# Layer 0 of a graph network: the end of the mixing moved from the counting stage into the graph products

## The chip, the cores and the metric

The kernel runs on one core of a Trainium2 chip. The metric is the device time of one execution in microseconds (us), as the median of several runs. The whole program has four layers; the change touches the first of them (layer 0) alone, which takes some 740 of the 3743 us.

The names of the engines in the profile: PE is the matrix engine (PEld its loads of weights), DVE the vector engine, ACT the scalar engine, POOL the GpSimd engine, SP the engine that only issues transfers. Each engine works off its instructions strictly in the order in which they stand in its queue.

## The reference

There are 3125 nodes with 256 features, and 100000 edges. Layer 0 begins like this (cut to what matters):

```
xn = layernorm(x)
x  = x + gnn(xn, edges) + mix(xn)
x  = x + ffn(layernorm(x))

gnn:  deg = number of edges of each node (src), loops added
      agg = sum over edges and loops of xn[dst] * deg[src]**-.5 * deg[dst]**-.5
      return relu(agg @ W.T + b)

mix:  z = rmsnorm(xn) ;  q, k, v = split(z @ w_qkv)          # 4 heads of 32
      q = softmax(q over a head's features) * 32**-.5 ;  k = softmax(k over nodes and memory)
      context = k . v ;  out = rmsnorm((q . context) @ w_out + b_out) * g_out
      return out + xn
```

## The kernel before

The nodes stand in 25 blocks of 125 (P); `x` and `xn` lie in the on-chip memory as 125 x 25 x 256, and most steps work on pieces of four blocks (`PIECES`: six pieces of 500 nodes and one of 125). The order in which the instructions of an engine stand is decided when the program is built, by a scheduler that goes by the dependences, the order in which the source issues them, and its own estimates of durations. `tc.issue_after(i)` keeps what stands inside it behind the instruction i on the same engine.

Layer 0 has four stages.

1. *Preparation* (`prep`). The edges are loaded, places in the edge list are searched (`junk`, `cnt`, `st`, and at line 404 `idx1`), and `x` is normalised piece by piece into `xn` (`l0_norm`) and turned into `xt` (`l0_unit`). When all of it is done and its memory is free, the edge records are gathered (line 456).

2. *Counting, with the mixing between* (`l0_first`: `counts` and `l0_mix_by_pieces`, interleaved by `together`, which always advances the part whose progress is smaller). For each of 25 target blocks b, `counts` builds one-hot rows of the edges (DVE, lines 507 and 510), multiplies them on PE (line 512), copies the result out with ACT (line 515, seven copies a block), turns it in four rounds through one bank of the accumulation memory (PE line 525, copied out in turn by DVE line 179 and ACT line 181), adds up degrees (line 530) and stores the turned counts in the memory off chip, `cnt_d[b]`, one row of blocks after another.
   The mixing first makes the context (`context`: the maxima of k, the sums over 25 blocks, and at its end `ctx_w`, which is the context times `w_out`, called `m2`). Then, for each piece, come the queries (lines 946 to 957), turned into `qt` (lines 961 and 964), and then what is called *the tail* here: for each block one matmul `qt` x `m2` (line 970), the addition of `b_out` (971), a square with its sum (ACT, 973); for each piece a square root (974), 975 and 976; for each block the scaling (979); for each piece `x += xn` (983, held behind line 957 by `issue_after`) and `x += t` (984).

3. *Weights of the graph layer* (`l0_gnn`, its first loop). `acc` = `xn` is overwritten by `xt` x W, scaled (PE line 279; DVE 616 or ACT 614), and then split into three bf16 parts, `y3` (lines 619 to 622).

4. *Graph products* (`l0_gnn`, its second loop). The 25 blocks of counts are read back (`cb`, line 629 through the helper lines 172 and 173 on SP's queue) in groups of 6, 6, 6 and 7 sources, in 12 buffers. For each group there are 25 steps h: 3 x m matmuls of 125 x 125 by 125 x 256 in bf16 into one bank (line 634), then the addition of the bank to `acc` on DVE (636). There are four such banks (`bank()`), shared with all other matmuls of the stage. In the last group a step also ends its block: lines 639 and 640, and for each finished piece, one piece later, the normalisation (lines 216 to 225), the turning (267, 179, 181) and the gates of the next part (279, 305, 1115, 1116).

Of the kernel before, what the change touches and what calls it, by code (L numbers as in the profile page):

```python
# [12 lines left out]
F32 = mybir.dt.float32  # L13
# [3 lines left out]
BF = mybir.dt.bfloat16  # L17
AF = mybir.ActivationFunctionType
OP = mybir.AluOpType
# [4 lines left out]
N = 3125  # L24
D = 256
# [92 lines left out]
PIECES3 = [(i, PW) for i in range(0, 4 * PW, PW)] + [(i, LW) for i in range(4 * PW, N, LW)]  # L118
NT = -(-N // 32) * 32
STORED = (4, 8, 12, 16, 20, 23, 25)  # L120
SOURCES = (6, 6, 6, 7)


class Net:
# [466 lines left out]
    def l0_gnn(self):  # L591

        nc = self.nc
        with ExitStack() as s:
            sb = s.enter_context(self.pool("g0_sb"))
            wk = s.enter_context(self.pool("g0_wk", 2))
            yb = s.enter_context(self.pool("g0_y", side="right"))
            w, bias = self.l0_w
            di = sb.tile([P, NB], F32, name="di")
            nc.scalar.activation(di, self.deg, AF.Sqrt)  # L600
            nc.vector.reciprocal(di, di)
            f = sb.tile([P, NB], F32, name="f")
            nc.vector.tensor_mul(f, di, self.len16)
            acc = self.xn
            y3 = yb.tile([P, NB, 3, D], BF, name="y3")
            for i, c in PIECES:
                b0, b1 = i // P, (i + c) // P
                for b in range(b0, b1):
                    if (b - b0) % 2 == 0:
                        ps = self.bank()  # L610
                    v = ps[:P, (b - b0) % 2 * D:][:, :D]
                    self.mm_tok(v, self.xt, b, w)
                    if b % 2:
                        nc.scalar.activation(acc[:, b, :], v, AF.Copy, scale=f[:, b:b + 1])
                    else:
                        nc.vector.tensor_scalar(acc[:, b, :], v, f[:, b:b + 1], None, op0=OP.mult)
                y, r = acc[:, b0:b1], wk.tile([P, 4, D], F32, name="r")[:, :b1 - b0]
                h0, h1, h2 = (y3[:, b0:b1, k, :] for k in range(3))
                nc.scalar.copy(h0, y)
                nc.vector.tensor_sub(r, y, h0)  # L620
                nc.scalar.copy(h1, r)
                nc.vector.tensor_sub(h2, r, h1)
            b0 = 0
            for m in SOURCES:
                cf = []
                for b in range(b0, b0 + m):
                    cb = wk.tile([P, N], BF, name="cb", bufs=2 * SOURCES[0])
                    self.move(nc.sync, cb, self.cnt_d[b])
                    cf.append(cb)
                for h in range(NB):  # L630
                    ps = self.bank()
                    for k in range(m):
                        for j in range(3):
                            nc.tensor.matmul(ps[:P, :D], cf[k][:, h * P:(h + 1) * P], y3[:, b0 + k, j, :],  # L634
                                             start=(k == 0 and j == 0), stop=(k == m - 1 and j == 2))
                    nc.vector.tensor_add(acc[:, h, :], ps[:P, :D], acc[:, h, :])  # L636
                    if b0 + m == NB:
                        t = acc[:, h, :]
                        nc.vector.scalar_tensor_tensor(t, t, di[:, h:h + 1], bias[:P], op0=OP.mult, op1=OP.add)
                        nc.vector.scalar_tensor_tensor(self.x[:, h, :], t, 0.0, self.x[:, h, :],  # L640
                                                       op0=OP.max, op1=OP.add)
                        if h % 4 == 3 or h == NB - 1:
                            self.arrive(h // 4 * PW)
                b0 += m
# [163 lines left out]
                nc.sync.dma_start(self.cnt_d[ds(b, 1)].rearrange("o p n -> (o p) n"), new)  # L808


    def context(self, sb, wk, w, wo, mem, share):


        nc = self.nc
# [47 lines left out]
        m2 = sb.tile([128, D], F32, name="ctx_w")  # L862
        nc.vector.tensor_scalar(m2, ps[:, :D], rz, 32 ** -0.5, op0=OP.mult, op1=OP.mult)
        return m2

# [36 lines left out]
                self.l0_norm(i, w)  # L902
                self.l0_unit(wk, r, i, w)

    def l0_first(self):

        with ExitStack() as s:
            csb = s.enter_context(self.pool("c_sb"))
            cwk = s.enter_context(self.pool("c_wk", 2))
            msb = s.enter_context(self.pool("m0_sb"))  # L910
            mwk = s.enter_context(self.pool("m0_wk", 2))
            pt = s.enter_context(self.pool("c_pt", 2, space=PSUM))
            px = s.enter_context(self.pool("c_px", 1, space=PSUM))
            py = s.enter_context(self.pool("c_py", 1, space=PSUM))
            mix = self.l0_mix_by_pieces(msb, mwk)
            next(mix)
            self.together([self.counts(csb, cwk, pt, px, py), mix])

    def l0_mix_by_pieces(self, sb, wk):
# [11 lines left out]
        bo = self.load_b(sb, "L0_mix_b_out")  # L931
        go = self.load_b(sb, "L0_mix_g_out")
# [5 lines left out]
        m2 = yield from self.context(sb, wk, w, wo, (mk, mv, mkt), 0.4)  # L938
        for i, c in PIECES:
            b0, n = i // P, c // P  # L940

            def part(f):
                return 0.4 + 0.6 * (i + f * c) / N

            ps = self.bank()
            for j in range(n):
                self.mm_tok(ps[:P, j * 128:(j + 1) * 128], self.xt, b0 + j, w[:, :, :128])
            q = wk.tile([P, 16, 32], F32, name="q")
            pq = ps[:P, :n * 128].rearrange("p (g d) -> p g d", d=32)
            qm = wk.tile([P, 16], F32, name="qm")  # L950
            nc.vector.tensor_reduce(qm[:, :4 * n], pq, axis=AX.X, op=OP.max)
            nc.vector.tensor_sub(q[:, :4 * n], pq, qm[:, :4 * n, None].to_broadcast([P, 4 * n, 32]))
            nc.scalar.activation(q[:, :4 * n], q[:, :4 * n], AF.Exp)
# [10 lines left out]
            nc.scalar.copy(qt[:, :c], ps[:, :c])  # L964
            yield part(0.6)
            t = wk.tile([P, 4, D], F32, name="t", bufs=1)
            ss = wk.tile([P, 4], F32, name="ss")
            for j in range(n):
                ps = self.bank()
                nc.tensor.matmul(ps[:P, :D], qt[:, j * P:(j + 1) * P], m2, start=True, stop=True)  # L970
                nc.vector.tensor_add(t[:, j, :], ps[:P, :D], bo[:P])
                sq = wk.tile([P, D], F32, name="sq")
                nc.scalar.activation(sq, t[:, j, :], AF.Square, accum_out=ss[:, j:j + 1])
            nc.scalar.activation(ss[:, :n], ss[:, :n], AF.Sqrt)
            nc.vector.tensor_scalar(ss[:, :n], ss[:, :n], 1e-12, 1.0 / 16, op0=OP.max, op1=OP.mult)
            nc.vector.reciprocal(ss[:, :n], ss[:, :n])
            yield part(0.9)
            for j in range(n):
                nc.vector.scalar_tensor_tensor(t[:, j, :], t[:, j, :], ss[:, j:j + 1], go[:P],
                                               op0=OP.mult, op1=OP.mult)  # L980
            v = self.x[:, b0:b0 + n, :]
            with self.tc.issue_after(weighed.ins):
                nc.vector.tensor_add(v, v, self.xn[:, b0:b0 + n])
            nc.vector.tensor_add(v, v, t[:, :n])
            yield part(1.0)

    def gen_l0_gnn(self):
        nc = self.nc
# [1898 lines left out]
    def run(self):  # L2887
# [5 lines left out]
        self.l0_first()  # L2893
        with self.pool("f0_g") as sb:
            self.l0_gates(sb)
            self.l0_gnn()
            first.__exit__(None, None, None)
            self.open_right()
            self.l0_ffn(True)
# [80 lines left out]
```

## Time and profile before

| | us |
|---|---|
| median of 3 runs (3740.36 to 3747.85) | 3740.75 |
| the profiled execution, its own time | 3745.47 |
| its span in the profile | 3743.2 |
| preparation, up to the first gather of records | 0 to 74.5 |
| counting and mixing; the last counts are stored at | 74.5 to 449.7 |
| weights, split and start of the products | 449.7 to 491.5 |
| products, groups of 6, at full rate | 491.5 to 631 |
| products, last group of 7 | 631 to 707 |

A row of groups by line reads: line, engine, operation, out<-in with partitions x elements, count | busy time, mean duration in ns | idle time of the engine just before them, and who ended it. A row of stretches reads: the stretch, its length, then for PE, PEld, DVE, ACT and POOL the busy time and (in brackets) the number of instructions, then the granted clock of the matrix engine as a share of the full one, the share of the transfer engines and GB/s. In the order of time a row begins with start and duration. A matmul in f32 shows as two records. Durations of instructions that follow each other closely overlap by some 0.08 us, so that a full queue advances by a little less than the duration shown.

### The profile page before, as it was taken

Reading aid. Unit: us, or ns where it says so; the run is one execution under the profiler, and the core shown is the slowest. Engines: PE = TensorE matmul, PEld = TensorE weight load, DVE = VectorE, ACT = ScalarE, POOL = GpSimd, SP = SyncE. Lnnn points to the kernel's source line nnn. Section 1 sums busy time; section 2 is a strip of 40 time slices with the busy share of each in tenths; the row PEclk is TensorE's granted clock in tenths of the full one; section 3 lists DMA queues with packets and bytes.
Section 4 is the critical chain, followed back from the end, with each engine's and each line's share of the span. In section 5 each row is a group of like instructions: output and inputs, shape, how many; then the busy total and the mean of one; then the engine's idle time right before and its main releaser. Section 6 shows DMA issues by size and latency. Waiting matters only on the chain. (4 is left out here: it accounts for less than half of the span.)

```text
span 3743.2 us, 61732 instructions
## 1 busy us (share of the span) xinstructions
PE 3319.3 (89%) x22027; PEld 2299.3 (61%) x22027; DVE 2406.5 (64%) x8119; ACT 1641.0 (44%) x3742; POOL 720.2 (19%) x702
## 2 busy tenths in 40 slices
PE   1888899789988979999998889998999999999978
PEld 1676699678866555555556677876663443444436
DVE  6878633875546673379246677886376666677663
ACT  3367510022225522222335566653247655556562
POOL 2000000054420340000003777772000000100011
PEclk9887699899989969999998899998999999999989
DMA  4144552346642110000003554545003222222135
GB/s 130 32 126 130 142 144 65 95 149 191 179 107 59 37 40 2 18 9 15 11 1 109 141 140 137 140 128 176 12 9 84 66 56 64 57 59 62 30 118 168
DMA packets 215084, 321.85 MB, mean 86 GB/s; under 512 B 51373, under 2 KB 158904, under 8 KB 214766
## 3 DMA queue, kind: packets, MB, share of 16 engines
q1 hardware_dynamic: 165308, 231.04, 21.5%
q0 software_dynamic: 40672, 83.85, 8.3%
q10 hardware_dynamic: 8786, 2.91, 0.4%
q8 instruction: 177, 2.90, 0.3%
q14 instruction: 141, 1.16, 0.1%
HBM read 248.17 MB, written 78.08 MB: 87 GB/s over the span
## 5 line engine op out<-in xcount | busy, mean ns | idle before, releaser
L2442 ACT ACTIVATE xn<-xn,us 125x1000 f32<-125x1000 f32 (+2 forms) x400 | 399.9, 1036 | 145.6 <-DVE z L2447 140.4
L2447 DVE SCALAR_TENSOR_TENSOR z<-xn,us,cs 125x1000 f32<-125x1000 f32 (+2 forms) x400 | 397.4, 1026 | 101.6 <-PE acc L2463 61.3
L2025 POOL DMA_INDIRECT hg<-hx_d,idx x405 | 403.5, 996 | 168.0 <-issue 99.3
L2463 PE MATMUL acc<-z,xr 125*32 125x500 f32 (+1 forms) x2800 | 368.7, 548 | 18.3 <-DVE z L2447 17.5
L1932 ACT ACTIVATE o<-ky,rest_d 128x50 bf16<-128x50 bf16 (+2 forms) x1190 | 302.9, 340 | 172.0 <-DVE ky L1923 149.3
L285 PE MATMUL ps<-xt,w 128*128 128x500 f32 (+1 forms) x672 | 274.7, 556 | 2.7 <-DMA w<-in_L_ffn_W_dram 1.6
L1655 DVE SCALAR_TENSOR_TENSOR x<-ps,lg,x 125x256 f32<-125x256 f32 x200 | 93.3, 483 | 245.4 <-PE ps L279 245.3
L2052 PE MATMUL acc<-hg,to 128*125 128x256 f32 x810 | 226.2, 422 | 11.5 <-DVE to L2048 10.7
L2463 PEld LDWEIGHTS acc<-z,xr 125*32 125x32 f32 x2800 | 100.1, 110 | 205.3 <-issue 116.9
L2463 PE MATMUL acc<-z,ones 125*32 125x500 f32 (+1 forms) x1400 | 224.9, 542 | 0.0
L634 PE MATMUL ps<-y,cb 125*125 125x256 bf16 x1875 | 210.6, 275 | 7.1 <-DVE xn L636 2.6
L634 PEld LDWEIGHTS <-cb 125*125 125x125 bf16 x1875 | 207.9, 138 | 7.7 <-issue 7.7
L285 PEld LDWEIGHTS ps<-xt,w 128*128 128x128 f32 x672 | 124.4, 198 | 116.0 <-issue 102.5
L279 PE MATMUL ps<-wo,h 128*125 128x256 f32 x800 | 187.8, 386 | 3.6 <-ACT h L1649 2.6
L1644 ACT ACTIVATE h<-ps,bnb,bng 128x500 f32<-128x500 f32 (+1 forms) x112 | 80.5, 722 | 248.6 <-PE ps L285 248.6
L2052 PEld LDWEIGHTS acc<-hg,to 128*125 128x125 f32 x810 | 156.5, 204 | 43.6 <-DVE to L2048 20.6
L279 PEld LDWEIGHTS ps<-wo,h 128*125 128x125 f32 x800 | 142.9, 187 | 65.8 <-ACT h L1649 43.5
L285 PE MATMUL ps<-h,w 128*128 128x500 f32 (+1 forms) x448 | 179.2, 541 | 1.4 <-ACT h L1644 1.0
L512 PE MATMUL t<-ky,lo 128*128 128x75 bf16 (+4 forms) x1251 | 140.6, 253 | 35.4 <-ACT ct L515 19.9
L515 ACT ACTIVATE ct<-t 125x500 bf16<-125x500 f32 (+4 forms) x175 | 137.0, 830 | 75.7 <-PE t L512 73.2
L285 PE MATMUL pl<-xbt,w 128*128 128x256 f32 x560 | 152.5, 402 | 10.0 <-ACT xbt L1271 9.2
L206 ACT ACTIVATE rstd_t<-rstd_t 125x4 f32<-125x4 f32 (+3 forms) x86 | 17.1, 202 | 301.6 <-DVE rstd_t L205 300.5
(696 smaller groups left out, 6902.9 us busy)
## 6 DMA issues: line engine op xcount, KB each, us to landing
w<-in_L_ffn_w_dram SPq DMA_DIRECT2D x70, 512.0 KB
cs<-ctt_d SPq DMA_DIRECT2D x100, 218.8 KB
lb<-low_d SPq DMA_DIRECT2D x76, 256.0 KB
w<-in_L_ffn_w_dram SPq DMA_DIRECT2D x18, 1024.0 KB
cnt_d<-cd SPq DMA_DIRECT2D x25, 683.6 KB
cb<-cnt_d SPq DMA_DIRECT2D x25, 683.6 KB
ctt_d<-ct SPq DMA_DIRECT2D x5, 2734.4 KB
cs<-ctt_d SPq DMA_DIRECT2D x50, 164.1 KB
```

What stands on the lines that cost most here:

```text
L279: self.nc.tensor.matmul(ps, xt[:, h, b * P:(b + 1) * P], w[:, h, :], start=(h == 0), stop=(h == k - 1))
L285: self.nc.tensor.matmul(ps, w[:, h, :], xt[:, h, i:i + n], start=(h == 0), stop=(h == k - 1))
L512: nc.tensor.matmul(t[:, w * 25 * r:(w + 1) * 25 * r], lo[:, :, n % 4], ky[:, :25 * r, n % 4], start=(j == 0), stop=(j == ws[w0 + w][2] - 1))
L515: nc.scalar.activation(ct[:, :, w0 * r:(w0 + m) * r].rearrange("p h (w r) -> p w h r", r=r), t[:P, :m * 25 * r].rearrange("p (w h r) -> p ...
L634: nc.tensor.matmul(ps[:P, :D], cf[k][:, h * P:(h + 1) * P], y3[:, b0 + k, j, :], start=(k == 0 and j == 0), stop=(k == m - 1 and j == 2))
L1655: nc.vector.scalar_tensor_tensor(self.x[:, b, :], ps[:P, :D], g[:, b, e:e + 1], self.x[:, b, :], op0=OP.mult, op1=OP.add)
L1932: nc.scalar.activation(o1[:, k], ky[:, :, i], AF.Copy, scale=rest[:, k, n + i:n + i + 1])
L2025: nc.gpsimd.indirect_dma_start(out=hg[:, j, :], out_offset=None, in_=hx, in_offset=bass.IndirectOffsetOnAxis(ap=idx[:, c0 + j - CF:c0 + j ...
L2052: nc.tensor.matmul(acc, to, hg[:, j, :D], start=(c == first[kind]), stop=(c == last[kind]))
L2442: nc.scalar.activation(t[:, :n], (tail if one else rows)[:P, h, :n], AF.Relu, bias=us[:, 2, b, h:h + 1], scale=us[:, 0, b, h:h + 1])
L2447: made.append(nc.vector.scalar_tensor_tensor(zs[h], t[:, :n], us[:, 1, b, h:h + 1], c, op0=OP.add, op1=OP.mult).ins)
L2463: mm = nc.tensor.matmul(out[q:q + 32, :w], left, zs[h0 + j][:, k * w:k * w + w], start=(b == 0), stop=(b == NB - 1), tile_position=(0, q))
```

## The change

- The tail of the mixing leaves the counting stage. All seven turned queries are kept in one tile of 128 x 3125 (`qt` in a new pool `m0_r`), with `m2`, `b_out` and `g_out`.
- In the graph products a generator, `l0_mixed`, is advanced once after each step h: four advances issue one block each (matmul, addition, square), the fifth issues the rest of the piece (root, scaling, `x += t`). With 32 advances it ends in the second group. The square is now written in bf16.
- `x += xn` becomes `l0_base` and is issued in the first loop of `l0_gnn`, before `acc` overwrites `xn`; there it stands in no `issue_after`.
- The sources come in five groups of five, in 9 buffers.

```diff
-SOURCES = (6, 6, 6, 7)
+SOURCES = (5, 5, 5, 5, 5)
...
             for i, c in PIECES:
+                self.l0_base(i, c)
                 b0, b1 = i // P, (i + c) // P
...
+            kept, *rest = self.l0_kept
+            mixed = (y for i, c in PIECES for y in self.l0_mixed(wk, i, c, kept[:, i:i + c], *rest, "r"))
...
-                    cb = wk.tile([P, N], BF, name="cb", bufs=2 * SOURCES[0])
+                    cb = wk.tile([P, N], BF, name="cb", bufs=2 * SOURCES[0] - 1)
...
                     nc.vector.tensor_add(acc[:, h, :], ps[:P, :D], acc[:, h, :])
+                    next(mixed, None)
...
-            qt = wk.tile([128, PW], F32, name="qt")
+            qt = kept[:, i:i + c] if keep else wk.tile([128, PW], F32, name="qt")
             nc.scalar.copy(qt[:, :c], ps[:, :c])
+            if keep:
+                yield part(1.0)
+                continue
...
+    def l0_base(self, i, c):
+        v, vn = (t[:, i // P:(i + c) // P] for t in (self.x, self.xn))
+        self.nc.vector.tensor_add(v, v, vn)
+
+    def l0_mixed(self, wk, i, c, qt, m2, bo, go, name="t"):
+        nc, b0, n = self.nc, i // P, c // P
+        t = wk.tile([P, 4, D], F32, name=name)
+        ss = wk.tile([P, 4], F32, name="ss")
+        for j in range(n):
+            ps = self.bank()
+            nc.tensor.matmul(ps[:P, :D], qt[:, j * P:(j + 1) * P], m2, start=True, stop=True)
+            nc.vector.tensor_add(t[:, j, :], ps[:P, :D], bo[:P])
+            sq = wk.tile([P, D], BF, name="sq")
+            nc.scalar.activation(sq, t[:, j, :], AF.Square, accum_out=ss[:, j:j + 1])
+            yield 0.4 + 0.6 * (i + j * P) / N
+        nc.scalar.activation(ss[:, :n], ss[:, :n], AF.Sqrt)
+        nc.vector.tensor_scalar(ss[:, :n], ss[:, :n], 1e-12, 1.0 / 16, op0=OP.max, op1=OP.mult)
+        nc.vector.reciprocal(ss[:, :n], ss[:, :n])
+        for j in range(n):
+            nc.vector.scalar_tensor_tensor(t[:, j, :], t[:, j, :], ss[:, j:j + 1], go[:P],
+                                           op0=OP.mult, op1=OP.mult)
+        v = self.x[:, b0:b0 + n, :]
+        nc.vector.tensor_add(v, v, t[:, :n])
+        yield 0.4 + 0.6 * (i + c) / N
```

In `run` the new pool is opened on the right side around `l0_first` and `l0_gnn`, and closed after the products.

More of the change, by code (lines that the diff above doesn't have):

```diff
@@ L808, in gen_counts, with context @@
                 nc.sync.dma_start(self.cnt_d[ds(b, 1)].rearrange("o p n -> (o p) n"), new)
-    def context(self, sb, wk, w, wo, mem, share):
+    def context(self, sb, wk, w, wo, mem, share, keep=None):
         nc = self.nc
@@ L861, in context @@
         nc.tensor.matmul(ps[:, :D], ct, wo[:, 0, :], start=True, stop=True)
-        m2 = sb.tile([128, D], F32, name="ctx_w")
+        m2 = (keep or sb).tile([128, D], F32, name="ctx_w")
         nc.vector.tensor_scalar(m2, ps[:, :D], rz, 32 ** -0.5, op0=OP.mult, op1=OP.mult)
@@ L903, in l0_prepare, with l0_first @@
                 self.l0_unit(wk, r, i, w)
-    def l0_first(self):
+    def l0_first(self, keep):
         with ExitStack() as s:
@@ L914, in l0_first, with l0_mix_by_pieces @@
             py = s.enter_context(self.pool("c_py", 1, space=PSUM))
-            mix = self.l0_mix_by_pieces(msb, mwk)
+            mix = self.l0_mix_by_pieces(msb, mwk, keep)
             next(mix)
             self.together([self.counts(csb, cwk, pt, px, py), mix])
-    def l0_mix_by_pieces(self, sb, wk):
+    def l0_mix_by_pieces(self, sb, wk, keep=None):
         nc, a = self.nc, self.a
@@ L930, in l0_mix_by_pieces @@
         wo = self.load_w(sb, "L0_mix_w_out", eng=nc.scalar)
-        bo = self.load_b(sb, "L0_mix_b_out")
-        go = self.load_b(sb, "L0_mix_g_out")
+        bo = self.load_b(keep or sb, "L0_mix_b_out")
+        go = self.load_b(keep or sb, "L0_mix_g_out")
         yield 0
@@ L937, in l0_mix_by_pieces @@
         self.searched = None
-        m2 = yield from self.context(sb, wk, w, wo, (mk, mv, mkt), 0.4)
+        m2 = yield from self.context(sb, wk, w, wo, (mk, mv, mkt), 0.4, keep)
+        if keep:
+            kept = keep.tile([128, N], F32, name="qt")
+            self.l0_kept = kept, m2, bo, go
         for i, c in PIECES:
@@ L962, in l0_mix_by_pieces @@
                                     self.ident[:P, :P])
-            qt = wk.tile([128, PW], F32, name="qt")
+            qt = kept[:, i:i + c] if keep else wk.tile([128, PW], F32, name="qt")
             nc.scalar.copy(qt[:, :c], ps[:, :c])
+            if keep:
+                yield part(1.0)
+                continue
             yield part(0.6)
[L966 to L981, printed above, removed]
-            with self.tc.issue_after(weighed.ins):
-                nc.vector.tensor_add(v, v, self.xn[:, b0:b0 + n])
@@ L984, in l0_mix_by_pieces @@
-            nc.vector.tensor_add(v, v, t[:, :n])
-            yield part(1.0)
+            with self.tc.issue_after(weighed.ins):
+                self.l0_base(i, c)
+            yield from self.l0_mixed(wk, i, c, qt, m2, bo, go)
+    def l0_base(self, i, c):
[21 more added lines that the diff above has]
+        yield 0.4 + 0.6 * (i + c) / N
@@ L2892, in run @@
         self.l0_w = self.load_w(gw, "L0_gnn_W"), self.load_b(gw, "L0_gnn_b")
-        self.l0_first()
+        mixed = self.pool("m0_r", side="right")
+        self.l0_first(mixed.__enter__())
         with self.pool("f0_g") as sb:
@@ L2896, in run @@
             self.l0_gnn()
+            mixed.__exit__(None, None, None)
             first.__exit__(None, None, None)
```

## The prediction

> **What bounds the kernel now.** First the stretches of layer 0, one row per stage (columns: PE, PEld, DVE, ACT, POOL busy, granted clock, transfer share, GB/s).
>
> ```profile
> 0.00:74.50 74.50, 15.16 (x58) 9.80 (x58) 46.59 (x164) 30.53 (x99) 13.71 (x24) 1.00 0.50 135
> ...
> 278.60:387.30 108.70, 85.88 (x865) 71.49 (x866) 91.57 (x247) 79.18 (x194) 0.42 (x2) 0.70 0.44 124
> 387.30:449.70 62.40, 49.07 (x427) 40.54 (x426) 45.58 (x117) 39.59 (x109) 0.21 (x1) 0.69 0.58 151
> ...
> 491.50:631.00 139.50, 139.49 (x1278) 139.49 (x1278) 30.68 (x73) 0.00 (x0) 0.00 (x0) 1.00 0.35 90
> 631.00:707.00 76.00, 73.22 (x649) 71.78 (x647) 59.12 (x226) 4.12 (x11) 0.00 (x0) 0.98 0.15 44
> ```
>
> To see: where the tail of the mixing runs (278.6 to 449.7), no engine is full; PE, DVE and ACT wait for each other. The products are PE and nothing else (1278 matmuls in 139.5 us, 0.109 each), until in the last group DVE is at 78%. Next, the groups of the tail between 276 and 446, and one line of the waits there:
>
> ```profile
> L970 PE MATMUL ps<-ctx_w,qt 128*125 128x256 f32 x50 | 23.5, 591 | 1.1 <-ACT qt L964 1.1
> L979 DVE SCALAR_TENSOR_TENSOR t<-t,ss,L_mix_g_out 125x256 f32<-125x256 f32 x25 | 10.9, 478 | 0.0
> L973 ACT ACTIVATE sq<-t 125x256 f32<-125x256 f32 x25 | 10.2, 414 | 2.0 <-DVE t L971 2.0
> L971 DVE TENSOR_TENSOR t<-ps,L_mix_b_out 125x256 f32<-125x256 f32 x25 | 10.1, 422 | 10.7 <-PE ps L970 10.6
> L974 ACT ACT_TABLE_LOAD x6 | 7.7, 1283 | 0.1
> L983 DVE TENSOR_TENSOR x<-x,xn 125x1024 f32<-125x1024 f32 x6 | 7.3, 1218 | 0.0
> L953 ACT ACT_TABLE_LOAD x5 | 6.4, 1283 | 0.1
> ...
> POOL ct L494 <- DMA ctt_d<-ct: 93.1, 2, 47.4
> ```
>
> These are durations, not the path: POOL's long wait costs nothing, since nobody waits for POOL there. Third, the order of time at the end of the preparation (DVE, then POOL), at the last load of a source (SP) and the first sums of the last group (DVE):
>
> ```profile
> 65.32 0.17 DVE L404 TENSOR_SCALAR idx<-st 128x10 int32<-128x10 f32 x1
> ...
> 74.47 0.94 POOL L456 DMA_INDIRECT g<-rec_d,idx  x1 [26.64 <-DMA L_gnn_W<-in_L_gnn_W_dram]
> ...
> 629.58 0.30 SPq L172 DMA_DIRECT2D cb<-cnt_d  x1
> ...
> 636.02 0.76 DVE L636 TENSOR_TENSOR xn<-ps,xn 125x256 f32<-125x256 f32 x2 [4.38 <-PE ps L634]
> ```
>
> **Preparation: +7.1 us.** `x += xn` depends on nothing but `x` and `xn`, and the `issue_after` is gone. In the built order of the changed kernel's DVE the six long additions stand inside the normalisation of pieces 1 to 5, all ahead of line 404; the seventh stands before the last `xt`. DVE is full there (from 27.7 to 65.3 it idles only 2.0 us, for ACT's roots). The gather waits for the whole preparation. An addition takes 1.22 us (line 983), 1.13 in a full queue: 6 x 1.13 + 0.33 = 7.1. Bounds: 5 if part falls into the roots' waits, 8.5 with nothing overlapped.
>
> **Counting: -36.6 us.** Out of it go, on DVE, lines 971, 975, 976, 979, 983, 984: 10.1 + 2.0 + 10.9 + 7.7 + 7.7 = 38.4 us; on ACT squares with their reads (15.1), roots (1.3), and all eleven table loads, as roots no longer alternate with exponentials: 30.5; on PE 23.5. What that is worth: blocks 11 to 24 end (first row of each store of `cnt_d`) between 278.55 and 449.71, 12.2 us a block. In the built order the mixing now ends within block 19; blocks 20 to 24 stand alone, as 21 and 24 nearly did: the last store to store took 10.4, and block 21 to 22 (first turn to first turn) 11.1, of which 0.8 was DVE at tail work when a copy was due. So five blocks at 10.3: their chain is serial, seven ACT copies of 0.8 and four rounds of turning. Blocks 11 to 19 keep the queries; without their tail they hold some 67 us of PE, 60 of DVE, 54 of ACT (85.9, 91.6 and 79.2 less the tail's share), for nine blocks. At PE 81% full, between this stage's 79% and the 86% DVE reaches with a full queue: 83 us, 9.2 a block, a little over the shortest now (8.0, from 379.3 to 387.3). 83 + 51.5 = 134.5 against 171.1. Bounds: 10.5 a block (only the waits go: -24) and 8.7 (-49).
>
> [...]
>
> **Start of the products: +6.7 us.** Weights and splits stay. But in the built order of PE two tail matmuls stand behind the first two steps' first source. With these two steps they hold all four banks, and DVE's additions that free them (old line 971) stand behind all splits, which end at 490.2. Today 72 matmuls are done by 491.5. Then: step 2 from 490.7, the third tail matmul, its release at 492.8, 33 matmuls x 0.109, the fourth tail matmul: step 4 begins at 496.9, 5.4 later, with 60 matmuls done, 12 x 0.109 = 1.3 fewer. Loads of sources are hidden here: the issues behind full queues stand 2.8 to 4 us apart from 469.9, so the fifth source is there by 483. Bounds: 3 and 8.
>
> **Products, up to the last group: +27.1 us.** The last group has five sources instead of seven, 375 matmuls instead of 525, so the groups before it hold 150 more: 150 x 0.109 = 16.4. Next to them, 21 tail matmuls remain in PE's stream: two records of 0.218 each (63 weight records in 13.76 us), 21 x 0.437 = 9.2. ACT is empty there, its 14 us of squares and roots are free. DVE: a piece takes about 8.5 us for five steps, with the wait for the root, against 9.8 of PE; the additions behind that wait hold banks, so 1.5 in all (0 to 4). Together 16.4 + 9.2 + 1.5 = 27.1, from 25.6 to 29.6. The transfers: a group's fifth source can only be loaded when the group before has ended with its buffer. The built order covers this: after the release 12 matmuls and 44 of the next four steps, 6.1 us. Today the 25th source has the same cover (issued 629.58, PE has 186 matmuls in every 20 us around it): nothing, if four later loads follow behind it. [...]
>
> **Last group: -2.4 us.** Five sources are 375 x 0.109 + 15.5 for turning and gates = 56 us of PE, but DVE's 59.1 us stays. The first sum is due at 5.3 (47 matmuls, four banks before the fifth source), and the waits for gates and roots that DVE has today (7.2 and 1.9) stay, as the built order puts PE's turning ahead of the next step: 5.3 + 59.1 + 9.1 = 73.5 against 75.9. Bounds: 66 (the gates' waits gone) and 78. So the groups of five return nearly nothing in time: PE's cover over DVE is gone. Behind this, the order is the old one on every engine, but for one pair of stores of `xn_d` which SP issues ahead of two loads of weights; both land long before use. POOL's order is the same.
>
> **Sum.** 7.1 - 36.6 + 6.7 + 27.1 - 2.4 = +1.9 us, on the profiled execution's own 3745.5 (its span is 3743.2; the 2.3 us around it stay). That run is 4.7 above the median, 3740.75; predicted is a median of 3742.6. What a measurement here can tell from no change is about 0.2%, 7.5 us.
>
> **Rivals.**
> *Slower: the counting stays serial (31%).* Place: lines 515, 525, 179, 181. For it: blocks alone already take 10.4, and the built order has the last five like that, with ACT and PE taking turns. Against: blocks of 8.0 to 8.8 exist. At 10.6 a block the stage gains 14 x 1.6 = 22 instead of 36.6, and the sum is +16: 3757. It decides from a mean of 10.0 on, where the stage gains 31 and the sum reaches the 7.5 us that can be told.
> *Slower: the fifth source comes late (5%).* The first load of a source took 5.3 us until the next could go (464.58 to 469.86), close to the cover of 6.1. Against: the 25th source today. If four boundaries lose 4 us each: 3759.
> *Faster: the counting becomes dense (26%).* PE, DVE and ACT are equally light, and the blocks take 8.7: -49, and the last group comes near 70, so 3.5 less: sum -14, 3727. Against: one bank for turning, ACT's 0.8 per copy.
> *No change to speak of (38%)*: what counting gives, preparation, start, tail matmuls and the unbalanced last group take back.
>
> **Numbers.** Predicted 3742.6. The terms' ends together (5 - 49 + 3 + 25.6 - 10 and 8.5 - 24 + 8 + 29.6 + 2) are -25 and +24; all at one end is unlikely, so the range is 3723 to 3762. Faster 0.26, same 0.38, slower 0.36.
>
> **What will show it.** Seven `x += xn` before 75 us, and the first gather at 81.6. The last counts stored near 420 (449.7 + 7.1 - 36.6), no table load between; if near 435, the serial rival. PE's step 4 some 47 us after that store, the last group beginning some 215 after it, with DVE over 80% busy and PE idle by about 15 us in it; today PE is idle by 2.8. A PE wait for `cb` at 4 boundaries would be the late source. I would be wrong altogether if the counting were bound by stores of `cnt_d` (one took 4.8 us to issue at 387.3), or if DVE's queue stalled PE by more than 4 us among the tail matmuls.

## The result

The changed kernel is slower: 3777.88 us (median of 5 runs, 3772.51 to 3785.35) against 3747.85 us of the kernel before (5 runs, 3740.36 to 3751.58), a ratio of 1.0093 (95% interval 1.0078 to 1.0107). The profiled executions took 3777.64 and 3745.47 us, with spans of 3775.5 and 3743.2. The prediction, +1.9 us with a range that ended at 3762, was wrong.

First the stretches of layer 0 in the profile after, matched to those shown of before: blocks 11 to 19 of the counting; blocks 20 to 24; products; last group.

```profile
291.50:403.20 111.70, 86.76 (x898) 76.25 (x898) 82.61 (x228) 68.74 (x168) 0.43 (x2) 0.73 0.42 121
403.20:457.30 54.10, 34.20 (x342) 28.45 (x342) 22.80 (x57) 25.05 (x66) 0.21 (x1) 0.50 0.66 173
...
500.00:674.00 174.00, 173.21 (x1531) 169.97 (x1530) 69.02 (x169) 13.04 (x53) 0.00 (x0) 0.99 0.29 73
674.00:745.00 71.00, 61.03 (x501) 58.42 (x499) 56.45 (x235) 4.90 (x13) 0.00 (x0) 0.93 0.17 49
```

Between the stores of blocks 10 and 24, the stage in which the tail stood, the kernel before kept DVE busy for 137.2 of 171.1 us (its two rows are in the prediction: 91.57 + 45.58). Now DVE is busy for 105.4 of 165.8. Its work shrank by 31.7 us and the stage by 5.3: most of what was taken out has become idle time. The groups of these stretches show where it went; first before (276 to 446), then after (286 to 457):

```profile
L507 DVE TENSOR_TENSOR lo<-i,keys 128x512 bf16<-128x512 bf16 x105 | 43.9, 418 | 2.6 <-PE t L512 2.2
L179 DVE COPY cd<-y 128x1000 bf16<-128x1000 bf16 x28 | 19.0, 680 | 9.7 <-PE y L525 9.1
L181 ACT COPY cd<-y 128x1000 bf16<-128x1000 bf16 x14 | 13.9, 989 | 17.9 <-PE y L525 17.9
```

```profile
L507 DVE TENSOR_TENSOR lo<-i,keys 128x512 bf16<-128x512 bf16 x107 | 44.8, 419 | 21.0 <-PE t L512 20.3
L179 DVE COPY cd<-y 128x1000 bf16<-128x1000 bf16 x30 | 20.4, 680 | 19.4 <-PE y L525 18.4 <-DMA cnt_d<-cd 0.8
L181 ACT COPY cd<-y 128x1000 bf16<-128x1000 bf16 x15 | 14.9, 992 | 35.6 <-PE y L525 23.0 <-issue 12.6
```

The instructions and their durations are the same; the idle time ahead of the one-hot rows and of the copies grew from 30.2 to 76.0 us, and 61.7 of the 76.0 are put down to waiting for PE. Before, DVE and ACT did the tail's work while a block waited for its turnings. Now they wait. The transfers are not what they wait for: their share is 0.42 and 0.66 in the two stretches, and DVE waited 0.8 us in all for a store of counts.

The balance, term by term, from the same marks in both profiles: the first gather of records, the last store of counts, the last sum of the group before the last (631.22 and 672.92), and the first activation after the gates (746.83 and 781.62).

| term | predicted | measured |
|---|---|---|
| preparation (gather at 74.47, then 81.28) | +7.1 | +6.8 |
| counting (gather to last store of counts: 375.2, then 376.1) | -36.6 | +0.8 |
| start and products up to the last group (181.5, then 215.6) | +33.8 | +34.1 |
| last group and gates (115.6, then 108.7) | -2.4 | -6.9 |
| all behind (2996.4, then 2993.9) | 0 | -2.5 |
| sum of spans | +1.9 | +32.3 |

Every term was nearly met but one, and that one was the whole gain. Its +0.8 is -5.3 in blocks 11 to 24, for which the forecast was made, and +6.1 in the stretch before them.

### The profile page after: what moved, and what is told of

Read it like the earlier page. It is cut to its first block, busy times and chain, and to the rows that moved or that the text cites. A ratio compares the mean times of both kernels' runs of the same rounds, so it can differ in the third digit from the quotient of the medians.

```text
span 3775.5 us, 61774 instructions
## 1 busy us (share of the span) xinstructions
PE 3325.4 (88%) x22027; PEld 2308.3 (61%) x22027; DVE 2413.1 (64%) x8144; ACT 1631.7 (43%) x3732; POOL 719.5 (19%) x702
## 5 line engine op out<-in xcount | busy, mean ns | idle before, releaser
L2072 PE MATMUL acc<-hg,to 128*125 128x256 f32 x810 | 218.9, 411 | 11.2 <-DVE to L2068 10.6
L637 PE MATMUL ps<-y,cb 125*125 125x256 bf16 x1875 | 217.2, 277 | 11.1 <-DVE r L993 6.7
L637 PEld LDWEIGHTS <-cb 125*125 125x125 bf16 x1875 | 211.6, 139 | 14.7 <-issue 12.0
L1282 POOL DMA_INDIRECT xb<-xn_d,sl_n x70 | 87.6, 1252 | 345.7 <-ACT t L1245 322.3
```

The source lines that it names most:

```text
L2072: nc.tensor.matmul(acc, to, hg[:, j, :D], start=(c == first[kind]), stop=(c == last[kind]))
```

## The experiments

They ran on another chip, on which the kernel before took 3964 to 3976 us (medians, and single runs where there was one); the 220 us more lie behind layer 0 (2996.4 us there in the first profile, 3215.8 on that chip), so that layer 0's stages can be compared, and whole times only within that chip. In three kernels layer 0 leaves other numbers to the later layers, and of those only the stages are used. All stages are gathered here, in us, each row from one profiled execution; the columns are the first gather, gather to block 10's store, blocks 11 to 19, blocks 20 to 24, both together, last store of counts to the first load of a source, and last store of counts to the first activation after the gates.

| kernel | gather | to 10 | 11-19 | 20-24 | 11-24 | to load | to gates |
|---|---|---|---|---|---|---|---|
| before | 74.5 | 204.1 | 108.7 | 62.4 | 171.2 | 14.9 | 297.1 |
| before, again | 75.3 | 212.1 | 108.6 | 62.4 | 171.0 | 17.1 | 297.1 |
| changed | 81.3 | 210.2 | 111.8 | 54.1 | 165.9 | 14.7 | 324.3 |
| changed, again | 80.8 | 210.7 | 114.8 | 53.8 | 168.6 | 16.2 | 327.5 |
| before, tail left out | 74.9 | 205.6 | 112.1 | 52.6 | 164.7 | 16.1 | 297.8 |
| changed, no queries | 80.7 | 215.8 | 96.1 | 54.0 | 150.1 | 16.4 | 325.0 |
| changed, two banks | 80.7 | 208.9 | 112.0 | 39.6 | 151.5 | 22.3 | 329.1 |
| changed, dummy turns | 80.8 | 210.7 | 106.9 | 55.2 | 162.1 | 16.5 | 327.2 |
| changed, two banks, no queries | 81.3 | 203.8 | 84.0 | 40.6 | 124.6 | 22.1 | 325.1 |
| changed, additions back | 74.6 | 207.3 | 111.6 | 53.0 | 164.6 | 16.6 | 327.1 |
| changed, last group of seven | 80.8 | 203.7 | 112.6 | 53.6 | 166.2 | 16.1 | 316.2 |
| changed, tail from sixth step | 81.3 | 204.1 | 111.9 | 53.7 | 165.5 | 16.1 | 319.8 |
| before, two banks | 74.6 | 205.0 | 107.8 | 54.7 | 162.6 | 22.2 | 301.9 |
| changed, mended | 74.6 | 201.2 | 111.7 | 41.1 | 152.8 | 22.2 | 311.4 |

### Both kernels again: how far a stage repeats

> The kernel before, unchanged, on the chip of the experiments, to see how far its stages repeat: gather at 74.5, blocks 10 to 24 in 168 to 174 (171.2 in the first profile), last store to first activation after the gates 296 to 302 (297.1). If blocks 10 to 24 came out at 180 or more, or at 164 or less, the differences of 5 us that I read between kernels would be of the size of the chance in one profile.

> The changed kernel, unchanged, on the same chip: gather at 81, blocks 10 to 24 in 164 to 168 (165.9), last store to first activation after the gates 324 to 329 (324.3). The same reading as for the kernel before: 160 or less, or 172 or more, in blocks 10 to 24 would put my differences in doubt.

The kernel before repeats to 0.2 us in blocks 11 to 24 and in the time to the gates; the changed kernel came 2.7 and 3.2 us longer, its 168.6 just outside the 164 to 168 that were expected. Among kernels whose counting is in the same order (changed, again, last group of seven, tail from sixth step) blocks 11 to 24 lie between 165.5 and 168.6. So differences of 5 us there can be read, and those under 3 us can't. The stretch up to block 10 can't be read so finely: 204.1 and 212.1 in the same kernel before, 203.7 to 210.7 in these four.

### What the tail cost where it stood

```diff
-            t = wk.tile([P, 4, D], F32, name="t", bufs=1)
-            ss = wk.tile([P, 4], F32, name="ss")
...
             yield part(0.9)
-            for j in range(n):
-                nc.vector.scalar_tensor_tensor(t[:, j, :], t[:, j, :], ss[:, j:j + 1], go[:P],
-                                               op0=OP.mult, op1=OP.mult)
...
-            nc.vector.tensor_add(v, v, t[:, :n])
```

> The kernel before, with the tail of the mixing left out of layer 0 (the matmul with m2, the bias, squares, root, scaling and x += t are not computed; x += xn stays where it was; everything else is the kernel before, six sources a group). It asks what the tail costs where it stood. Measure: the distance from the store of counts of block 10 to that of block 24, 171.2 us before, 165.9 after. Theory 'free filler' (a block is set by its own chain of matmul, copy and turning, and the tail lay in the gaps of that chain): 163 to 170. Theory 'new order' (the tail did cost some 35 us, but the changed kernel's order of queries and counts lost it again): 150 or less.

Measured: 164.7 us. Taking all of the tail away, with nothing put anywhere, shortens the stage by 6.5 us (171.2 to 164.7), though it takes 25 us of work from DVE (137.2 to 112.0 busy), 24 from ACT (118.8 to 94.3) and 13 from PE (134.9 to 122.0). That is what "free filler" expected. But it doesn't rule out "new order", since the queries moved in this kernel too. The turnings of the queries on PE, one per block, show it; blocks 11 to 19 of the kernel before, then of the changed kernel:

```profile
L961 PE MATMUL ps<-ident,q 125*128 125x125 f32 x16 | 3.9, 392 | 0.2 <-DVE q L957 0.2
```

```profile
L968 PE MATMUL ps<-ident,q 125*128 125x125 f32 x25 | 6.0, 371 | 2.4 <-DVE q L964 2.4
```

Before, four of the seven queries lay in blocks 11 to 19 and three in blocks 20 to 24. In the changed kernel, and in this one with the tail left out (also 25 turnings), all seven lie in blocks 11 to 19. So 6.5 us is the price of the tail together with that move. The next run gives a bound for the tail alone.

### What a block costs alone

```diff
-            qt = kept[:, i:i + c] if keep else wk.tile([128, PW], F32, name="qt")
-            nc.scalar.copy(qt[:, :c], ps[:, :c])
             if keep:
-                yield part(1.0)
-                continue
-            yield part(0.6)
+                nc.gpsimd.memset(kept[:, i:i + c], 0.0)
+            yield part(1.0)
```

(with the lines ahead of it, from the query's matmuls to its turning, also left out)

> The changed kernel, with the queries left out of the counting (the kept queries are zeros; matmuls, softmax and turning of q are not computed), so that blocks 11 to 24 are counts alone. Same measure, 165.9 us in the changed kernel. Theory 'free filler', a block has a floor of its own near the 10.8 us that blocks 20 to 24 show: 14 x 10.8 = 151, at a granted clock near half. Theory 'the three engines share the work' (as the prediction had it, time follows busy time; the queries hold PE some 24, DVE 28 and ACT 12 us): near 165.9 - 30 = 136 or less.

Measured: 150.1 us, 10.7 a block. With tail and queries both gone, the fourteen blocks still take 150 of 171 us. So the tail cost at most some 21 us where it stood (171.2 less 150.1), however the queries lie. The forecast of 134.5 us for this stage lay 15.6 us below what the counts take with nothing beside them.

```profile
296.60:392.70 96.10, 69.28 (x765) 60.49 (x765) 64.24 (x187) 59.48 (x150) 0.42 (x2) 0.52 0.49 140
392.70:446.70 54.00, 34.21 (x342) 28.48 (x342) 22.79 (x57) 25.07 (x66) 0.21 (x1) 0.50 0.68 174
```

In these two stretches together (blocks 11 to 19 and 20 to 24 of this kernel) PE is at 69%, DVE at 58% and ACT at 56%, and the transfers at 0.49 and 0.68: nothing is full, and the clock is at 0.52 and 0.50.

### Chain or clock

How a block spends its 12 us is seen in the order of time of the changed kernel. From the store of block 22, at 434.2, to 438.9 ACT makes the seven copies of block 23 (line 515), with the multiplications of the one-hot rows between them. Then comes the turning of block 23, up to its store:

```profile
439.08 1.02 PE L525 MATMUL y<-ident_b,ct 125*128 125x125 bf16 x8
...
441.02 0.67 DVE L179 COPY cd<-y 128x1000 bf16<-128x1000 bf16 x1
441.75 1.02 PE L525 MATMUL y<-ident_b,ct 125*128 125x125 bf16 x8 [1.21 <-DVE cd L179]
...
442.86 0.99 ACT L181 COPY cd<-y 128x1000 bf16<-128x1000 bf16 x1 [4.01 <-issue]
443.90 1.00 PE L525 MATMUL y<-ident_b,ct 125*128 125x125 bf16 x8 [0.96 <-ACT cd L181]
...
444.93 0.68 DVE L179 COPY cd<-y 128x1000 bf16<-128x1000 bf16 x1 [3.24 <-PE y L525]
445.67 0.27 PE L525 MATMUL y<-ident_b,ct 125*128 125x125 bf16 x1 [0.58 <-DVE cd L179]
445.97 0.27 ACT L181 COPY cd<-y 128x125 bf16<-128x125 bf16 x1 [2.12 <-PE y L525]
446.26 0.31 SPq L172 DMA_DIRECT2D cnt_d<-cd  x1
```

Four times PE turns into the one bank, one engine copies, and PE waits for the copy before the next round: 7.2 us in which each engine mostly waits for another. Eight turnings take 1.02 us here, at a clock of 0.50 (PE is busy for 34.2 of the 54.1 us of blocks 20 to 24), and took 0.60 in the kernel before at 447.74, at a clock of 1.00. So two causes were to be told apart: the one bank, and the clock. A second bank was made of the one that the keys had used:

```diff
-                x = py.tile([128, 8, 128], BF, name="y")
+                x = py.tile([128, 8, 128], BF, name="y") if h0 % 16 == 0 else px.tile([128, 8, 128], BF, name="x")
```

> The changed kernel, with a second bank for the turning of the counts: the bank that the keys used takes every other round. Same measure, 165.9. Theory 'chain' (the one bank makes each round of turning wait for the copy of the round before): each block saves two to three waits of 0.7 to 1.3 us, 2 to 3 us a block, so 125 to 145, and blocks 0 to 10 gain too. Theory 'clock' (PE's steps are long because the clock falls to half when PE idles): the blocks stay within 5 us of 165.9, since idle PE stays idle PE.

and, apart from that, PE was kept busy with turnings that nobody reads:

```diff
+                if b > 10 and m == 8:
+                    z = px.tile([128, 8, 128], BF, name="x")
+                    for h in range(12):
+                        nc.tensor.transpose(z[:, h % 8, :P], turned[:, h0 + h % 8, :], self.ident_b[:P, :P])
                 self.evac(cd[:, h0:h0 + m, :], x[:, :m, :P])
```

> The changed kernel, with twelve more turnings per round of eight into an unused bank in blocks 11 to 24, whose results nobody reads: PE gets more work, 36 x 0.077 to 0.128 = 2.8 to 4.6 us a block, most of it in the waits for the copies. Same measure, 165.9, and the granted clock, 0.73 and 0.54 in the two stretches of the tail of the counting. Theory 'clock': the clock rises to 0.85 or more, PE's own steps shrink by some 3 us in a block alone, and the stage gets shorter, 150 to 160, in spite of the added work. Theory 'chain': the clock may rise, but the copies and waits stay, and the added work makes the stage longer, 166 to 185.

The windows of blocks 11 to 19 and 20 to 24, first with two banks, then with the dummy turns:

```profile
289.70:401.60 111.90, 86.29 (x929) 75.77 (x928) 84.40 (x234) 70.44 (x172) 0.42 (x2) 0.74 0.42 120
401.60:441.20 39.60, 30.33 (x339) 25.91 (x337) 22.73 (x57) 25.32 (x66) 0.21 (x1) 0.67 0.76 209
```

```profile
291.50:398.40 106.90, 95.07 (x1247) 86.62 (x1248) 83.20 (x229) 68.07 (x168) 0.43 (x2) 0.90 0.46 126
398.40:453.60 55.20, 45.39 (x499) 39.64 (x497) 22.85 (x57) 25.34 (x68) 0.21 (x1) 0.72 0.67 171
```

With the second bank the stage takes 151.5 us, longer than the 125 to 145 of the chain theory. Where blocks stand alone it takes 54.1 to 39.6 us, 10.8 to 7.9 a block, and PE's waits for a copy ahead of a turning fall from 13.2 to 0.8 us: there the one bank is the limit. The dummy turns raise the clock from 0.73 to 0.90 and from 0.50 to 0.72, and the blocks alone get no shorter (54.1 to 55.2). Blocks 11 to 19 gain 4.9 us. In all that is 162.1, between the two expectations (150 to 160 for the clock, 166 to 185 for the chain). The added turnings stand in the same queue, so this is a faster clock net of 36 more turnings a block; what the clock is worth alone was not measured. It does not bring the stage to the 150 to 160 us of the clock theory. (The clock of 0.54 in that text is 0.50 in the row of blocks 20 to 24.)

But in the nine blocks with queries the second bank brought nothing (111.8 to 112.0), against the chain theory, which promised 2 to 3 us for each block. So the second bank was tried with the queries left out:

> The changed kernel, with the second turning bank and with the queries left out (zeros in their place), block 10 to 24: 165.9 us in the changed kernel, 150.1 without queries, 151.5 with the second bank. Theory 'chain': with two banks all fourteen blocks take the 7.9 us of blocks 20 to 24 in the second-bank run, 111 to 120. Then the nine blocks with queries are not bound by the turning but by the place of the queries in the queues, 30 to 40 us of it. Rival: another limit (stores of counts, the copies) holds these blocks at 9.5 or more, 133 to 150.

Measured: 124.6, between the two. Blocks 11 to 19 go to 84.0 us, 9.3 each, and blocks 20 to 24 stay at 40.6. So the second bank works in those nine blocks too, once the queries are gone, and the queries then cost 28.0 us (112.0 less 84.0), against 15.7 with one bank (111.8 less 96.1). They hold PE for 16.9, DVE for 17.8 and ACT for 7.7 us there (the differences of the two kernels' windows). Why 18 us of work cost 28 us when the bank is no longer the limit is seen in part on PE, in the kernel with two banks and queries:

```profile
378.79 1.35 PE L512 MATMUL t<-ky,lo 128*128 128x125 bf16 x10
382.57 0.65 PE L968 MATMUL ps<-ident,q 125*128 125x125 f32 x4 [2.42 <-DVE q L964]
...
388.87 1.09 PE L968 MATMUL ps<-ident,q 125*128 125x125 f32 x4 [3.91 <-DVE q L964]
...
392.55 0.62 PE L512 MATMUL t<-ky,lo 128*128 128x125 bf16 x4 [1.73 <-ACT ct L515]
```

The last three queries follow one upon the other, each waiting for its own softmax on DVE, and for 12.4 us (380.1 to 392.5) no one-hot row is multiplied. That points to the place of the queries in the queues; no run changed that place alone.

### Two smaller prices: the additions and the start

`x += xn` was put back behind the weighted query of its piece:

```diff
-                self.l0_base(i, c)
                 b0, b1 = i // P, (i + c) // P
...
             if keep:
+                with self.tc.issue_after(weighed.ins):
+                    self.l0_base(i, c)
                 yield part(1.0)
```

> The changed kernel, with x += xn put back into the counting, behind the weighted query of its piece, as in the kernel before. If the preparation's 6.8 us (first gather of records at 81.28 against 74.47 us) are these additions and nothing else, the gather starts at 74.5 again. Theory 'free filler': the additions lie in DVE's gaps in the counting, so the last counts are stored 5 to 8 us earlier, at 449 to 452, and the ratio to the kernel before falls from 1.0093 to about 1.0075. Rival, that DVE's 7.3 us count in full wherever they stand: last store at 456 to 458 and no gain.

The gather started at 74.6, and blocks 11 to 24 stayed at 164.6: the seven additions cost 6.7 us ahead of the gather and nothing in the counting. The last store came at 446.5, a little earlier than expected, as the stretch to block 10 was 2.9 us shorter than in the profile of the changed kernel. The ratio is 1.0055 (95% interval 1.0034 to 1.0076), which just holds the 1.0075 that was expected.

For the start, the moved tail was advanced from the sixth step on:

```diff
-                    next(mixed, None)
+                    if b0 or h > 4:
+                        next(mixed, None)
```

> The changed kernel, with the moved tail advanced from the sixth step of the products on instead of the first, so that no tail matmul stands among the first sources. From the last store of counts to the first activation after the gates (324.3 us in the changed kernel, 325.0 to 329.1 in the runs with the same products). If the first tail matmuls hold two of the four banks behind DVE's splits, as the prediction has it, 4 to 6 us less than its neighbours: 319 to 323. Rival, that PE waits for the split itself and the banks don't matter: 324 to 328.

Measured: 319.8, inside the expected 319 to 323, against 324.3 in the changed kernel and 327.5 in the same kernel on the same chip. The order of time on PE shows the mechanism. First the changed kernel, then this one:

```profile
486.49 0.37 PE L637 MATMUL ps<-y,cb 125*125 125x256 bf16 x1 [0.98 <-DVE y L623]
...
497.64 2.08 PE L637 MATMUL ps<-y,cb 125*125 125x256 bf16 x9 [5.87 <-DVE r L993]
...
505.76 3.44 PE L637 MATMUL ps<-y,cb 125*125 125x256 bf16 x30
```

```profile
480.29 9.38 PE L637 MATMUL ps<-y,cb 125*125 125x256 bf16 x58 [0.99 <-DVE y L623]
492.33 5.10 PE L637 MATMUL ps<-y,cb 125*125 125x256 bf16 x30 [2.66 <-DVE xn L639]
```

PE waited 5.87 us for an addition of the tail (line 993), which stood on DVE behind all the splits but the last, short one: its matmul had ended at 487.7, the addition began at 497.2. (The engines kept to their queues: in both profiles the records of PE, DVE and ACT up to 707 us follow the built order line by line, in the kernel before through 519, 1191 and 242 stretches of one line each.) Without tail matmuls among the first sources the longest wait is the 2.66 us for DVE that the kernel before had as well (2.61).

### The last group

```diff
-SOURCES = (5, 5, 5, 5, 5)
+SOURCES = (5, 4, 5, 4, 7)
```

> The changed kernel, with the sources in groups of 5, 4, 5, 4 and 7 in the same nine buffers. From the last store of counts to the first activation after the gates it takes 289.8 us before and 324.3 in the changed kernel. My reckoning of this 34.5: tail matmuls 9.2, start of the products 5 to 6, and the rest, 13 to 20, is PE idle in the last group of five, as DVE bounds it. If so, groups that end with seven give back 10 to 14 us: 310 to 314, ratio 1.0055 to 1.0065. Rival: with seven sources in nine buffers two of the last seven can only be loaded after the group before, PE waits for them, and the gain is 5 us or less.

The numbers 289.8 and 34.5 in that text are slips of mine: the kernel before takes 746.83 - 449.71 = 297.1 us, and the difference to be explained is 27.2. Measured: 316.2 us, 8.1 to 11.3 less than the same products in groups of five (324.3 to 327.5). That is more than the rival allowed and 2 us short of what was expected from the mechanism. Ratio 1.0068 (1.0048 to 1.0089). In this kernel the load of the last two sources, issued after the release, from 648.8 us on, was hidden (from 640 to 770 PE does not wait for a source), but the first sum of the last group comes late: DVE waits 8.27 us for it, against 4.71 in the changed kernel.

### Can it be mended, and the second bank for the kernel before

> The changed kernel with everything that the runs point to: x += xn back in the counting, the second turning bank, groups of 5, 4, 5, 4 and 7, and the moved tail advanced from the sixth step on, so that no tail matmul stands among the first sources. If the terms add: additions -6.8, second bank -14.4, groups -12, start -5, in all -38 against the changed kernel, so 3 to 10 us below the kernel before, ratio 0.997 to 0.999. Rival: the parts overlap (the additions fill what the second bank freed), the sum is -25 and the ratio 1.001 to 1.003.

> The kernel before with the second turning bank alone. Blocks 19 to 24 took 62.4 us with the tail between them; in the changed kernel the second bank brought 54.1 to 39.6 where blocks stand alone, and nothing (111.7 to 111.9) where queries lie between. Theory 'chain': the gaps in which the tail lay get shorter, so it is no longer free: block 10 to 24 goes from 171.2 to 158 to 166, ratio 0.997 to 0.9985. Rival, that the work between the blocks keeps them at 12 us: 169 to 173, ratio 0.9995 to 1.001.

The kernel before with two banks: ratio 0.9994 (0.9971 to 1.0016). Its counting gets 8.6 us shorter in blocks 11 to 24, as the chain theory says, but no time can be told to be gained. The mended kernel, with additions back, second bank, groups of 5, 4, 5, 4, 7 and the later start together: 1.0011 (0.9992 to 1.0031). Its profiled execution, 3954.2 us, is near the fastest of its ten (3951.91 to 3984.07, median 3967.79): there it is at the gates at 740.0 us, against 746.8 and 755.5 in the two profiles of the kernel before and 781.6 and 787.5 in those of the changed one, and 3 to 11 us of that lie in the stretch to block 10, which differs by as much from one execution to the next. Neither beats the kernel before; the ratio of the mended one is that of the rival in its text (1.001 to 1.003), not the 0.997 to 0.999 of terms that add.

Where both lose is seen in the last two columns of the table. With two banks the last counts are stored 7 to 21 us earlier, but the first source is loaded 22.2 us after that store instead of 15 to 17, and from there on the loads are late. In the mended kernel (PE, in order of time):

```profile
457.59 0.40 PE L636 MATMUL ps<-y,cb 125*125 125x256 bf16 x2 [4.15 <-DMA cb<-cnt_d]
...
464.15 1.50 PE L636 MATMUL ps<-y,cb 125*125 125x256 bf16 x12 [1.78 <-DMA cb<-cnt_d]
467.48 1.50 PE L636 MATMUL ps<-y,cb 125*125 125x256 bf16 x12 [1.84 <-DMA cb<-cnt_d]
470.83 4.77 PE L636 MATMUL ps<-y,cb 125*125 125x256 bf16 x42 [1.86 <-DMA cb<-cnt_d]
```

and on SP's queue, the last stores of counts and what lies between them and the first source:

```profile
428.54 1.14 SPq L172 DMA_DIRECT2D cnt_d<-cd  x1
...
434.70 6.49 SPq L173 DMA_DIRECT2D ctt_d<-ct  x1
441.30 1.42 SPq L188 DMA_DIRECT2D L_ffn_gate_w<-in_L_ffn_gate_w_dram  x1
450.76 0.32 SPq L172 DMA_DIRECT2D cb<-cnt_d  x1
```

SP waits 7.3 us here for a store of a row of blocks (`ctt_d`, up to 2.7 MB each) to land, against 5.2 us in the kernel before. The stores, and from 450.8 on the loads of the sources, fill the transfers: their share from 428.5 to 475 is 0.99. PE waits 9.6 us in all for sources (8.4 in the kernel before with two banks), where the kernel before shows no such wait in its first profile and 1.6 us in its second. The limit of this passage has moved from the counts to their transport.

## Why the prediction was wrong

*Preparation* (+7.1 predicted, +6.8 measured) was right, and by its mechanism: line 983 runs seven times between 35.6 and 76.2 us, and with the additions back the gather starts at 74.6.

*Counting* (-36.6, measured +0.8, of which -5.3 in blocks 11 to 24) is the step that failed, and in it one sentence: "At PE 81% full ... 83 us, 9.2 a block" for blocks 11 to 19. They took 111.8 us. The five blocks alone were well forecast, 51.5 against 54.1. Two things were wrong in the sentence.

The first is the floor. The sentence treated the nine blocks as a stage in which time follows busy time. But a block has a chain of its own, counts, copies and four rounds through one bank, which takes 10.7 us with nothing beside it, and in which PE is idle for 31%, DVE and ACT for over 40%. With no query at all PE is busy for 69.3 us in blocks 11 to 19, near the 67 of the forecast, and they take 96.1 us instead of 83. The tail lay in the gaps of this chain and could be had for 6.5 us, the move of the queries included, and for some 21 at most.

The second is the work. The prediction gave these blocks 67 us of PE, 60 of DVE and 54 of ACT; the row after has 86.8, 82.6 and 68.7. It put the end of the mixing within block 19, but took the work from the old stretch, which held only four of the seven queries; three more moved in, and one-hot rows too (84 steps of line 507 instead of 76). It also took some 80% of the tail out of that stretch (18.9 of 23.5 us on PE), where only 16 of the 25 blocks of the tail lay in it (14.8 us on PE). By the prediction's own 81%, the 86.8 us that PE really holds would have given 107 us, and a gain of 12 us for the whole stage instead of 36.6. Of the 28.8 us by which the sentence missed, 13.1 are there without any query, and the queries bring the other 15.7.

The profile of before held what was needed for the floor. I read it for the five last blocks (10.4 and 11.1 us where a block was nearly alone), and for the nine others took comfort from the shortest block, 8.0. That was misread: the stores of counts come in turns, 15.9 and 8.5, 16.8 and 8.3, 14.0 and 8.8 us apart, so that a short distance is the other half of a long one, and two of them make 23 to 25. Had the 10.4 been applied to all fourteen blocks, 146 us would have been the floor and 25 us the most that could be gained by taking out all of the mixing, queries and all. The rival "serial" had the right mechanism and too low a price: at 10.6 a block for all fourteen it left out that the queries come on top, and blocks 11 to 19 took 12.4 each. The lower gain of the range, -24, should have been near zero.

The granted clock did not make up for this. In the kernel before it is 0.70 and 0.69 in the two stretches; it was 1.00 from 342.0 to 350.8, where 96 PE records took 7.81 us, and 0.50 from 411.0 to 422.7, where 80 took 8.71. In the changed kernel PE is less busy, 121.0 instead of 134.9 us in blocks 11 to 24, and the clock is at 0.73 in blocks 11 to 19 and at 0.50 through all of blocks 20 to 24. With the dummy turns it was 0.90 and 0.72, and blocks 11 to 24 took 3.8 us less, net of the added turnings.

*Start* (+6.7) and *products* (+27.1): 33.8 together, 34.1 measured. Leaving the tail out of the first steps gave 4.5 us against one profile of the changed kernel and 7.7 against the other, around the 6.7. The trace also gives the term itself. The 61st matmul of a source begins at 505.76, 48.4 us after the last store, where 47.2 were forecast; in the kernel before the 73rd begins 41.8 us after it. With the 12 matmuls between (1.3 us) that makes 7.9 for the start, and leaves 26.2 for the products, inside both ranges (3 to 8, 25.6 to 29.6). The 9.2 us of tail matmuls and the 16.4 us of moved sources were not measured one by one. From 500 to 674 PE is busy for 173.2 of 174.0 us and waits for no source: the fifth source of a group was never late. With nine buffers PE waited for a source at none of the four boundaries, where the rival of the late fifth source had 4 us at each.

*Last group* (-2.4, measured -6.9): inside its range of -10 to +2. To its last sum it took 67.2 us where 73.5 were forecast. The waits together were no shorter than forecast: 7.9 us for sums (5.3 forecast) and 7.6 for gates (9.1 with the roots). The term that was too large is DVE's 59.1 us, which "stays": DVE was busy for 52.6. In a fuller queue its instructions overlap, two sums taking 0.76 us where one takes 0.42; that this is all of the difference was not tried. PE is idle for 10.0 us in it (71.0 less 61.0), where 15 were expected.

## What to carry to other kernels

Work that fills the gaps of another part's chain can be nearly free where it stands, however much of an engine it holds; the price of taking it out is read by asking how long the chain takes alone, not by subtracting busy time. Look for a stretch of the profile in which the chain does stand alone, and apply its time to every block before any gain is written down. Where the new order moves other work into a stretch, count that work by the new order, not by the old profile. And when distances between events alternate, long and short, only the sum of a pair is a duration.

## What the runs showed of the hardware that I had not expected

With PE busy for 34.2 of 54.1 us, in pieces of up to some two us, the granted clock stayed at 0.50 for the whole stretch; 36 more turnings a block brought it to 0.72, with PE busy for 45.4 of 55.2. The same instruction order can differ by 8 us in the stretch from the gather to block 10 from one execution to the next (204.1 and 212.1 in the kernel before). In the first profiles of the two kernels blocks 1 to 4 (from the store of block 0 to that of block 4) took 68.3 us at a clock of 0.69 to 1.00, and 73.4 us at 0.59 to 0.83, with the same numbers of PE instructions but one; that it is the clock which varies there was not tried.
